# Neighbour slots two at a time: 16-bit words, shift and mask in place of one comparison per slot, and spaced indirect DMAs

## The chip, the core and the metric

The kernel runs on one core of a Trainium2 chip. The metric is the device time of one execution in microseconds (us). Its engines are PE (matmuls), DVE (VectorE), ACT (ScalarE), POOL (GpSimd) and SP (SyncE, which only starts DMAs here).

## The reference

Sixteen graphs of 1024 nodes with 64 channels go through two layers. The first is where the change lies:

```
h = relu(layernorm(x))                           # per node, 64 channels
# drop every skip-th neighbour, and the same edges from the other side
nb   = number of neighbours;  skip = ceil(nb / 2) if nb > 10 else 1
rem  = neighbour and skip > 1 and rank % skip == skip - 1;  rem |= rem.T
nd   = (adjacency with the node itself) and not rem
# per node and channel, over the kept neighbours' h, sorted:
s    = sort(where(nd, h[neighbour], inf));  nv = nd.sum()
agg  = 0.25 * quantile(s, .25) + 0.5 * quantile(s, .5) + 0.25 * quantile(s, .75)   # interpolated
x    = x + mlp(h + agg) * mask                   # 64 -> 128 -> 64
```

The second layer is a layer norm, three graph convolutions `relu(adj @ (x W) + b)` with batch norm, a linear layer over their concatenation, and a residual. A node has some 16 neighbours on average and at most 42 kept ones here; the sort over neighbours is most of the work.

## The kernel before

**Pairs and places.** The graphs are handled in eight pairs, so that 2 x 64 channels fill 128 partitions. `prepare(p)` loads a pair's adjacency, transposes it on PE, drops neighbours, counts each node's kept neighbours (`nv`) and orders the nodes by that count: a node's rank is its *place*. The rows of the adjacency are scattered to DRAM by place (`live_d`, L894, on POOL), read back and transposed (`liveT`). Nodes with like counts then lie next to each other, and ranges of places get a fixed number of neighbour *slots*:

| places | slots | how the neighbours' rows are brought |
|---|---|---|
| block 0: 0 to 200 | 11 | one-hot matmuls |
| block 1: 200 to 392 | 13 | one-hot matmuls |
| block 2: 392 to 640 | 15 | one-hot matmuls |
| NODES: 640 to 768, 768 to 896, 896 to 960 | 17, 19, 21 | indirect DMAs |
| MID: 960 to 1008; tail: 1008 to 1024 | 26; 42 | one-hot matmuls |

**Numbers of neighbours.** At the end of `prepare`, `find_live` multiplies `liveT` with a triangular matrix that has `LIVE` = 128 on its diagonal. In the product `pr` (PSUM, one column a place) a kept neighbour whose rank in its column is k has the value 129 + k, every other node a value under 129. ACT copies the columns of places 0 to 640 (`SPLIT`) as bf16 to `st.r[0]` (L987, once for each of 2 graphs x 8 chunks of 128 nodes and pair: 128 times), and those from 960 on to `st.r[1]` (L1000).

**One-hot gathering.** `gather` takes the slots of a block in groups of as many as fit one PSUM tile (two for blocks 0 and 1, one for block 2). For each slot DVE compares `r` with 129 + slot over all chunks that can hold it:

```
nc.vector.tensor_scalar(                                                    # L1149
    s[:, k, :, us, w0:], r[:, :, us, at + w0 : at + W], float(LIVE + 1 + k0 + k), None, ALU.is_equal
)
```

PE multiplies the features `hp` (h as a sum of three bf16 parts) with that one-hot matrix and adds up over chunks and parts in `pg` (L1180). A place without a neighbour in this slot gets a large number by another product (`none`, L1169 and L1174). ACT copies `pg` to the sorting buffer `g` (L1185). `fewer` (`w0`) leaves out columns in which no node has that slot; where the first product doesn't cover the tile, a product with an identity's zero block clears it (L1159).

**Indirect gathering.** For NODES, lists of row numbers are made (`list_rows`, L711 to L731 on DVE), and `fetch_nodes` issues on POOL one indirect DMA for each slot and half a (L1293; 744 in all, in 20 jobs in the order of `NODE_ORDER`). All jobs but three late ones write into one buffer (tag `gn`), so a job's first DMA waits until the sort of the job before it has read its last. The DMA of the first half (a = 0) also waits for the latest instruction of a sorting network issued so far (`sorted_by`), so that the requests are spread. `list_rows` and all of this precede the sort of the same rows.

**Sorting.** `quantiles` runs a sorting network of DVE minima and maxima (L1087) over `g` and multiplies and adds the quantiles' coefficients (L1099, L1108).

**Order.** `weave(sort, *others)` steps through a sort, and after each part of it issues as many steps of the other generators as are due by the sort's share of work. The number of steps of a gather is what `gather_block` returns. The main loop over p does, in this order: sort block 0 with gathering of block 1 and asking for NODES rows; sort NODES with gathering of block 2; the next fetch, with the sorts of blocks 1 and 2 and gathering of MID and tail; sort NODES; the next fetch, with the sort of MID (`sort_pairs`) and gathering of the next pair's block 0. `prepare(p + 1)` is spread over the first five by `SHARES`. The framework's scheduler then sets each engine's order from this program. After the seventh round, `later` (second layer) is woven with the last pair's sorts: `load` fetches each graph's aggregates back by place with 8 indirect DMAs on POOL (L1486), `first_layer` (L1383) and `next_layer` (L1426 to L1445) follow.

In `load` and in `ask` nothing makes one indirect DMA wait for another, apart from the limited number of semaphores.

Of the kernel before, what the change touches and what calls it, by code (L numbers as in the profile page):

```python
# [13 lines left out]
F8 = mybir.dt.float8e4  # L14
I32 = mybir.dt.int32
U8 = mybir.dt.uint8
U32 = mybir.dt.uint32
AF = mybir.ActivationFunctionType
ALU = mybir.AluOpType
# [388 lines left out]
def graph_layers_kernel(ctx: ExitStack, tc: tile.TileContext, ins, out: bass.AP):  # L408
# [229 lines left out]
    def prepare(p, pools):  # L638


        work, keep, ps = pools
        st = Pair()
        st.p = p
        room = work.tile([P, 4, 2, NT, C], F32, tag="stays", name="room")
        xt, h, sq = room[:, 0], room[:, 1], room[:, 2].rearrange("p x t c -> p (x t) c")
        for x in range(2):
            nc.sync.dma_start(out=xt[:, x], in_=rows_of(x_d[2 * p + x]))
        flat = "p x t c -> p (x t) c"
        layernorm_relu(work, h.rearrange(flat), xt.rearrange(flat), sq, T2)
        for x in range(2):  # L650
            nc.sync.dma_start(out=rows_of(h_d[2 * p + x][:, :]), in_=h[:, x])
            for t in range(4):
                row0 = x * ROWS + 2 + 256 * t
                nc.sync.dma_start(
                    out=rows_d[p][row0 : row0 + 256, :].rearrange("(u j) c -> j u c", j=32),
                    in_=h[32 * t : 32 * t + 32, x],
                )
        yield
        st.g = {}
        st.nvs = keep.tile([P, HELD], BF16, tag="nvs", bufs=2, name="nvs")  # L660
        r0 = keep.tile([P, 2, NT, SPLIT], BF16, tag="r0", name="r0")
        r1 = keep.tile([P, 2, NT, N - REST], BF16, tag="r1", name="r1")
        st.r = (r0, r1)
        rows = {}
        fetch, find_live = [None] * 2, [None] * 2

        def first_rows():
            rows[0] = fetch[0]()

        for x in range(2):  # L670
            fetch[x], find_live[x] = yield from prepare_one(st, x, pools, first_rows if x else None)
        rows[1] = fetch[1]()
        yield
# [12 lines left out]
        nc.vector.tensor_scalar(half, st.nvs, 0.498, MAGIC, ALU.mult, ALU.add)  # L686
        nc.vector.tensor_scalar(half, half, MAGIC, None, ALU.subtract)
        for q, (tau, _) in enumerate(TAUS):
            nc.vector.scalar_tensor_tensor(st.z[:, q, :], st.nvs, -tau, half, ALU.mult, ALU.add)
        yield  # L690

        h = work.tile([P, 2, NT, C], F32, tag="a", bufs=2, name="h_again")
        for x in range(2):
            nc.sync.dma_start(out=h[:, x], in_=rows_of(h_d[2 * p + x][:, :]))
        st.hp = keep.tile([P, 3, 2, NT, C], BF16, tag="hp", name="hp")
        nc.scalar.copy(st.hp[:, 0], h)  # L696
        nc.vector.tensor_tensor(h, h, st.hp[:, 0], ALU.subtract)
        nc.scalar.copy(st.hp[:, 1], h)
        nc.vector.tensor_tensor(st.hp[:, 2], h, st.hp[:, 1], ALU.subtract)
        yield  # L700
        return st
# [62 lines left out]
    def prepare_one(st, x, pools, ahead=None):  # L764
# [156 lines left out]
        def find_live(lp_all, listed):  # L921
# [55 lines left out]
            for u in range(NT):  # L977
                pr = ps.tile([P, N], F32, tag="big", bufs=2, name="pr")
                for a in range(0, SPLIT, HALF):
                    o = slice(a, min(a + HALF, SPLIT))  # L980
                    nc.tensor.matmul(out=pr[:, o], lhsT=upto, rhs=liveT[:, u, o], start=True, stop=(u == 0))
                    if u:
                        nc.tensor.matmul(
                            out=pr[:, o], lhsT=before[:, u : u + 1].to_broadcast([P, P]), rhs=sums[:, o],
                            start=False, stop=True,
                        )
                nc.scalar.copy(st.r[0][:, x, u, :], pr[:, :SPLIT])  # L987
                if u % 2:
                    yield
            def number_rest():  # L990

# [29 lines left out]
    def view(bufs, spec, n1, n2, inner=None):  # L1021

        first, s1, s2 = spec
        buf, base = (bufs[1], first - OTHER) if first >= OTHER else (bufs[0], first)

        def dim(n, s):

            return n, s

        ap = buf[:, base, :]  # L1030
        W = ap.shape[-1]
        t = ap.ap if not callable(ap.ap) else ap.ap()
        part, last = list(t)[0], list(t)[-1]
        dims = [list(part)]
        if n1 > 1:
            dims.append([s1 * W, n1])
        if n2 > 1:
            dims.append([s2 * W, n2])
        if inner is None:
            dims.append(list(last))  # L1040
        else:
            dims += [[s2 * W, n2]] * (n1 == 1 and n2 == 1) + [[inner, W // inner], [1, inner]]
        return bass.AP(tensor=ap.tensor, offset=ap.offset, ap=dims)

    plans = {}
    sorted_by = [None]
# [69 lines left out]
    def per_group(block):  # L1116

        W = block[1] - block[0]
        return max(1, min(HALF // W, 400 // W))

    def gather(st, block, g, pools):


        work, ps, _ = pools
        j0, j1, least, slots = block
        first, end, fewer = NEAR[(BLOCKS + (TAIL,)).index(block)]
        W = j1 - j0
        high = missing_high(slots, least)
        r, at = (st.r[0], j0) if j1 <= SPLIT else (st.r[1], j0 - REST)
        per = per_group(block)  # L1130
        for k0 in range(0, slots, per):
            if k0:
# [85 lines left out]
    def gather_block(st, n, pools, home=None, into=None, first=-0.2, end=0.9):  # L1218


        work, ps, rows = pools
        block = (BLOCKS + (TAIL,))[n]
        j0, j1, _, slots = block
        pool, tag, bufs = home or (rows, f"g{n % 2}", 1)

        def groups():
            if n >= MID:
                z = part_z[n]
                nc.scalar.copy(z[:, :, st.p % z.shape[2], :], st.z[:, :, slice(*held(block))])
            to = into  # L1230
            if to is None:
                to = st.g[n] = pool.tile([P, slots, j1 - j0], F32, tag=tag, bufs=bufs, name="g")
            send(pools, (yield from gather(st, block, to, pools)))
            in_place = n == MID or st.p == NP - 1
            if n >= MID and not in_place:
                nc.scalar.dma_start(out=part_d[n][st.p][:, :, :], in_=to)

        return Steps(groups()), -(-slots // per_group(block)), first, end

    def sort_block(st, n, pools):  # L1240

# [38 lines left out]
    def fetch_nodes(pairs, i, pools, tag):  # L1280
# [7 lines left out]
        def ask():  # L1288
            for k in range(slots):
                for a in range(G):  # L1290
                    st = pairs[a if i == 2 else 0]
                    at = 4 if i == 2 else 2 * a + i
                    asked = nc.gpsimd.indirect_dma_start(  # L1293
                        out=g[:, k, a * C : (a + 1) * C],
                        out_offset=None,
                        in_=rows_d[st.p][:, :],
                        in_offset=bass.IndirectOffsetOnAxis(ap=st.listed[:, at, k : k + 1], axis=0),
                    )
                    if a == 0 and sorted_by[0] is not None:
                        tc.add_manual_dep(  # L1300
                            asked.ins, sorted_by[0].ins.name,
                            mybir.DependencyInfo(mybir.DependencyClass.Sync, mybir.DependencyReason.DATA),
                            reason="rows are asked for one by one",
                        )
                yield

        z = work.tile([P, len(TAUS), G], F32, tag="z_nodes", bufs=2, name="z_nodes")
# [161 lines left out]
    def later(pools, keep, done):  # L1469
# [4 lines left out]
        def load(p):  # L1474
# [5 lines left out]
            for x in range(2):  # L1480
# [2 lines left out]
                nc.sync.dma_start(out=h[:, :, x, :], in_=rows_of(h_d[b][:, :]))  # L1483
                with tc.high_priority():
                    for t in range(NT):
                        nc.gpsimd.indirect_dma_start(  # L1486
                            out=agg[:, t, x, :],
                            out_offset=None,
                            in_=agg_d[b][:, :],
                            in_offset=bass.IndirectOffsetOnAxis(ap=place[:, b, t : t + 1], axis=0),  # L1490
                        )
                nc.sync.dma_start(out=mk[:, :, x], in_=mask_d[b])
            return xt, h, agg, mk

# [329 lines left out]
```

## Time and profile before

| | |
|---|---|
| median of 3 runs | 2872.86 us (2872.21 to 2877.92) |
| profiled execution | 2872.55 us, span 2870.7 us |
| DVE busy | 2347.0 us, 82% of the span |
| PE busy | 2095.5 us, 73% |
| ACT busy | 1584.5 us, 55% |
| POOL busy | 1517.0 us, 53% |
| granted PE clock, mean | 0.88 |

The profile is of one execution. The span runs from its first instruction to its last; the time has some 2 us around it. "Busy" counts an engine's instructions, not its waits. A row of a group reads: line, engine, operation, output <- input with partitions x elements and type, count | busy us, mean ns of one | idle us just before them and what ended that idle time. In the rows of 40 slices each digit is the busy share in tenths of a slice of 71.8 us.

### The profile page before, as it was taken

How to read it: one execution, taken by the hardware profiler on the slowest of the kernel's cores; microseconds unless marked ns; L12 is line 12 of the kernel's file. 1: busy time of each engine (PE TensorE's matmuls, PEld its weight loads, DVE VectorE, ACT ScalarE, POOL GpSimd, SP SyncE). 2: the span in 40 equal slices, each digit the busy share in tenths (PEclk: the TensorE clock that was granted, in tenths of full speed). 3: DMA queues.
4: the chain of work that ended last, by engine and by line, in shares of the span. 5: the costliest groups of instructions: out<-in, count | busy, mean ns of one | idle time of the engine just before them, and what ended most of it. 6: DMA issues, size and time to landing. Idle time of an engine off the chain costs nothing.

```text
span 2870.7 us, 59053 instructions
## 1 busy us (share of the span) xinstructions
PE 2095.5 (73%) x23402; PEld 1450.2 (51%) x23402; DVE 2347.0 (82%) x5475; ACT 1584.5 (55%) x3316; POOL 1517.0 (53%) x1155
## 2 busy tenths in 40 slices
PE   1576986996888688778744985898488396437868
PEld 0344763674565366447522663675366263224545
DVE  3217999999989999999999999999699396637943
ACT  2775776687468568847762687588333133122222
POOL 5115374475838546572834275655855748862220
PEclk9888997998999799889966997999798798768989
DMA  3313222332322242233230322322310341211221
GB/s 98 107 33 103 82 77 58 110 89 65 95 74 73 59 116 86 57 79 99 77 77 12 104 89 74 111 74 64 79 26 14 76 82 52 41 39 45 61 60 46
DMA packets 261055, 205.57 MB, mean 72 GB/s; under 512 B 217121, under 2 KB 217249, under 8 KB 256673
## 3 DMA queue, kind: packets, MB, share of 16 engines
q1 hardware_dynamic: 165120, 131.39, 15.8%
q0 software_dynamic: 39680, 62.23, 9.0%
q10 hardware_dynamic: 55968, 8.09, 1.7%
q8 instruction: 185, 3.03, 0.4%
q14 instruction: 102, 0.83, 0.1%
HBM read 148.82 MB, written 52.75 MB: 70 GB/s over the span
## 4 chain that ended last, share of the span: by engine, by line
DVE 31%; PE 13%; POOL 8%; DMA 8%; ACT 7%; issue 4%; ACTq 0%; POOLq 0%; DVEq 0%; SPq 0%
DVE s L1149 5%; DVE t L1087 4%; POOL g_nodes L1293 4%; PE pg L1441 4%; POOL agg L1486 4%; DVE t_nodes L1087 3%; PE pg L1180 3%; DVE g L1087 2%; DVE g_pairs L1087 2%; DVE t_pairs L1087 2%; DMA a<-in_adj 2%; DVE g_nodes L1087 2%; ACT stays L883 2%; DMA g_nodes<-rows_d,rows_listed 2%; DMA agg<-agg_d,place 2%
## 5 line engine op out<-in xcount | busy, mean ns | idle before, releaser
L1293 POOL DMA_INDIRECT g_nodes<-rows_d,rows_listed x744 | 1123.2, 1510 | 874.4 <-DVE prod L1099 312.5
L1180 PE MATMUL pg<-s,hp 128*64 128x248 bf16 (+6 forms) x12048 | 883.0, 299 | 206.2 <-DVE s L1149 151.1
L1180 PEld LDWEIGHTS <-hp 128*64 128x64 bf16 x12048 | 645.6, 113 | 383.0 <-ACT hp L696 76.4
L1149 DVE TENSOR_SCALAR s<-r 128x3200 bf16<-128x3200 bf16 (+19 forms) x856 | 407.4, 525 | 25.9 <-PE pg L1180 23.7
L1441 PE MATMUL pg<-adjT,xw 128*64 128x512 fp8e4 x2304 | 279.1, 391 | 39.9 <-ACT xw L1430 32.7
L894 POOL DMA_INDIRECT live_d<-edge,place x128 | 189.4, 1480 | 146.9 <-DVE place L886 109.1
L1486 POOL DMA_INDIRECT agg<-agg_d,place x128 | 139.0, 1086 | 190.7 <-DMA agg_d<-agg_nodes 59.1
L1441 PEld LDWEIGHTS <-xw 128*64 128x64 bf16 x2304 | 135.7, 112 | 165.3 <-ACT xw L1430 39.6
L1185 ACT COPY g<-pg 128x248 f32<-128x248 f32 (+3 forms) x238 | 97.0, 408 | 213.1 <-PE pg L1180 212.3
L781 ACT ACTIVATE edge<-a 128x1024 fp8e4<-128x1024 uint32 x128 | 135.5, 1058 | 92.3 <-DMA a<-in_adj 75.5
L788 PE MATMUL ptE<-ident_h,one 128*128 128x128 bf16 x1024 | 84.8, 233 | 114.9 <-DVE one L785 69.2
L1087 DVE TENSOR_TENSOR t<-g 128x800 f32<-128x800 f32 (+9 forms) x184 | 167.5, 923 | 0.8
L1087 DVE TENSOR_TENSOR g<-t 128x992 f32<-128x992 f32 (+7 forms) x176 | 160.2, 931 | 2.0
L864 ACT ACTIVATE edge<-q,bias 128x1024 fp8e4<-128x1024 f32 x128 | 142.2, 1112 | 31.4 <-PE q L859 31.1
L1383 DVE TENSOR_TENSOR agg<-agg,h_late 128x1024 f32<-128x1024 f32 x8 | 9.8, 1229 | 182.2 <-DMA agg<-agg_d,place 182.2
L883 ACT ACTIVATE stays<-keys,minus 128x1024 fp8e4<-128x1024 f32 x128 | 143.1, 1118 | 27.2 <-PE keys L875 26.1
L837 ACT ACTIVATE stays<-cs,back 128x1024 f16<-128x1024 f32 x128 | 137.5, 1113 | 28.3 <-PE cs L833 17.0
L791 ACT ACTIVATE edgeT<-ptE 128x1024 fp8e4<-128x1024 f32 x128 | 131.2, 1028 | 15.5 <-PE ptE L788 14.6
L788 PEld LDWEIGHTS <-one 128*128 128x128 fp8e4 x1024 | 66.0, 104 | 140.2 <-DVE one L785 86.3
L1087 DVE TENSOR_TENSOR t_nodes<-g_nodes 128x256 f32<-128x256 f32 (+6 forms) x192 | 124.2, 658 | 14.4 <-DMA g_nodes<-rows_d,rows_listed 13.8
L929 PE MATMUL pt<-ident_h,lp 128*128 128x128 bf16 x1024 | 88.2, 239 | 58.9 <-ACT liveT L932 30.2
L1445 ACT ACTIVATE xT<-pg,c_L_gnn_b 128x512 f32<-128x512 f32 x48 | 32.9, 686 | 176.6 <-PE pg L1441 176.6
(245 smaller groups left out, 4622.2 us busy)
## 6 DMA issues: line engine op xcount, KB each, us to landing
a<-in_adj SPq DMA_DIRECT2D x128, 512.0 KB
adjT_d<-edgeT SPq DMA_DIRECT2D x16, 1024.0 KB
lp<-live_d POOLq DMA_DIRECT2D x32, 512.0 KB
adjT<-adjT_d SPq DMA_DIRECT2D x16, 1024.0 KB
g_nodes<-rows_d,rows_listed POOLq DMA_INDIRECT x744
room<-in_x SPq DMA_DIRECT2D x16, 256.0 KB
h_d<-room SPq DMA_DIRECT2D x16, 256.0 KB
rows_d<-room SPq DMA_DIRECT2D x64, 64.0 KB
```

The costliest lines, as they stand in the source:

```text
L781: nc.scalar.activation(edge[:, t, :], a[:, :].bitcast(U32), AF.Sign, accum_out=found[:, 0, b, t : t + 1], saturate=False)
L788: nc.tensor.matmul(out=pt[:, u, :], lhsT=one[:, u * P : (u + 1) * P], rhs=ident_h, start=True, stop=True)
L837: nc.scalar.activation(stays[:, t, :], cs, AF.Abs, bias=back[:, t : t + 1], scale=2.0)
L864: nc.scalar.activation(edge[:, t, :], q, AF.Relu, bias=bias(-2.0), accum_out=nv[:, t : t + 1], saturate=False)
L883: nc.scalar.activation(junk, keys, AF.Sign, bias=minus[:, t : t + 1], accum_out=above[:, t : t + 1], saturate=False)
L894: sent = nc.gpsimd.indirect_dma_start(out=live_d[b][:, :], out_offset=bass.IndirectOffsetOnAxis(ap=place[:, b, t : t + 1], axis=0), in_=ed ...
L1087: sorted_by[0] = nc.vector.tensor_tensor(view(bufs, o, n1, n2), view(bufs, a, n1, n2), view(bufs, b, n1, n2), ALU.max if op else ALU.min)
L1149: nc.vector.tensor_scalar(s[:, k, :, us, w0:], r[:, :, us, at + w0 : at + W], float(LIVE + 1 + k0 + k), None, ALU.is_equal)
L1180: summed = nc.tensor.matmul(out=pg[x * C : (x + 1) * C, ks, w0:], lhsT=st.hp[:, part, x, u, :], rhs=s[:, ks, x, u, w0:], start=(whole and ...
L1293: asked = nc.gpsimd.indirect_dma_start(out=g[:, k, a * C : (a + 1) * C], out_offset=None, in_=rows_d[st.p][:, :], in_offset=bass.IndirectO ...
L1441: nc.tensor.matmul(out=pg[cs, :], lhsT=part[:, u, cs], rhs=adjT[x][:, u, sl], start=(u == 0 and k == 0), stop=(u == NT - 1 and k == len(xw ...
L1486: nc.gpsimd.indirect_dma_start(out=agg[:, t, x, :], out_offset=None, in_=agg_d[b][:, :], in_offset=bass.IndirectOffsetOnAxis(ap=place[:, b ...
```

## The change

Four things change.

1. `st.r[0]` holds 16-bit integers. ACT writes `Relu(128 * pr - 256)` to it, rounded to an integer: for a kept neighbour of rank k this is 128 * (127 + k), which is the bit pattern of the bf16 number 2^k. After every second chunk a second ACT instruction reads these words as bf16 and writes them as integers in place: the word is then 1 << k, with 0 or low values for other nodes.
2. Blocks 0 to 2 are gathered by `gather_words`. DVE shifts the words by |k - 3| (right for k over 3, left below) and masks with 0x0808. The low byte is 8 where the rank is k, the high byte where it is k + 8; read as fp8, 8 is 2^-6. One DVE instruction serves slots k and k + 8; slots without a partner keep one instruction each. PE reads every second byte as its moving operand, and ACT's eviction multiplies by 64 (an ACTIVATE with `Copy` and a scale, in place of a COPY). Each block is done in groups of two slots, or one. Full widths are used: `fewer` and the clearing products aren't.
3. In `ask`, the first half's DMA of every odd slot from 3 on waits for the last DMA of the slot before; in `load`, the fifth of eight DMAs waits for the fourth.
4. The step count that `gather_block` gives `weave` becomes slots - 8 + (17 - slots) // 2: 6, 7 and 8 for blocks 0, 1 and 2, where it was 6, 7 and 15.

The tail and MID keep the comparison.

```diff
-        r0 = keep.tile([P, 2, NT, SPLIT], BF16, tag="r0", name="r0")
+        r0 = keep.tile([P, 2, NT, SPLIT], U16, tag="r0", name="r0")
...
-                nc.scalar.copy(st.r[0][:, x, u, :], pr[:, :SPLIT])
+                nc.scalar.activation(
+                    st.r[0][:, x, u, :], pr[:, :SPLIT], AF.Relu, bias=bias(-2.0 * 128.0), scale=128.0
+                )
                 if u % 2:
+                    words = st.r[0][:, x, u - 1 : u + 1, :]
+                    nc.scalar.copy(words, words.bitcast(BF16))
                     yield
...
+    def gather_words(st, block, g, pools):
...
+        groups = [((k,), slice(k, k + 9, 8)) for k in range(slots - 8)]
+        groups += [(tuple(range(k, min(k + 2, 8))), slice(k, min(k + 2, 8))) for k in range(slots - 8, 8, 2)]
+        for at, (shifts, of) in enumerate(groups):
+            if at:
+                yield
+            ks = range(slots)[of]
+            n = len(ks)
...
+            s = work.tile([P, len(shifts), 2, NT, W], U16, tag="s", bufs=2, name="s")
+            for j, k in enumerate(shifts):
+                mine = chunks if len(shifts) == 1 else chunks[j : j + 1]
+                us = slice(min(c.start for c in mine), max(c.stop for c in mine))
+                nc.vector.tensor_scalar(
+                    s[:, j, :, us, :], st.r[0][:, :, us, j0:j1], abs(k - 3), 0x0808,
+                    ALU.logical_shift_right if k > 3 else ALU.logical_shift_left, ALU.bitwise_and,
+                )
+            by_byte = s[:, :, :, :, :].bitcast(F8).rearrange("p j x u (w h) -> p j h x u w", h=2)
+            pg = ps.tile([P, n, W], F32, tag="pg", bufs=3, name="pg")
...
+                those = slice(those[0], those[-1] + 1)
+                for part in range(3):
+                    for x in range(2):
+                        picked = by_byte[:, 0, those, x, u, :] if len(shifts) == 1 else by_byte[:, those, 0, x, u, :]
+                        summed = nc.tensor.matmul(
+                            out=pg[x * C : (x + 1) * C, those, :], lhsT=st.hp[:, part, x, u, :], rhs=picked,
+                            start=(i == 0 and part == 0), stop=(i == len(looks) - 1 and part == 2),
+                        )
+            nc.scalar.activation(g[:, of, :], pg, AF.Copy, scale=64.0)
...
     def gather(st, block, g, pools):
+        if block[1] <= SPLIT:
+            return (yield from gather_words(st, block, g, pools))
...
-        return Steps(groups()), -(-slots // per_group(block)), first, end
+        steps = slots - 8 + (17 - slots) // 2 if j1 <= SPLIT else -(-slots // per_group(block))
+        return Steps(groups()), steps, first, end
...
                     if a == 0 and sorted_by[0] is not None:
-                        tc.add_manual_dep(...)
+                        wait_for(asked, sorted_by[0])
+                    if a == 0 and k % 2 and k > 1:
+                        wait_for(asked, last)
+                    last = asked
...
-                        nc.gpsimd.indirect_dma_start(
+                        asked = nc.gpsimd.indirect_dma_start(
...
+                        if t == 4:
+                            wait_for(asked, last)
+                        last = asked
```

More of the change, by code (lines that the diff above doesn't have):

```diff
@@ L16 @@
 U8 = mybir.dt.uint8
+U16 = mybir.dt.uint16
 U32 = mybir.dt.uint32
@@ L1043, in view, with wait_for @@
         return bass.AP(tensor=ap.tensor, offset=ap.offset, ap=dims)
+    def wait_for(one, other):
+        tc.add_manual_dep(
+            one.ins, other.ins.name,
+            mybir.DependencyInfo(mybir.DependencyClass.Sync, mybir.DependencyReason.DATA),
+            reason="indirect DMAs come with pauses",
+        )
     plans = {}
@@ L1119, in per_group @@
         return max(1, min(HALF // W, 400 // W))
+    def gather_words(st, block, g, pools):
+        work, ps, _ = pools
+        j0, j1, least, slots = block
+        first, end, _ = NEAR[BLOCKS.index(block)]
+        W = j1 - j0
+        high = missing_high(slots, least)
+        groups = [((k,), slice(k, k + 9, 8)) for k in range(slots - 8)]
[5 more added lines that the diff above has]
+            n = len(ks)
+            chunks = [
+                range(
+                    max([c for c in first if k >= first[c]], default=0),
+                    min([c for c in end if k < end[c]], default=NT),
+                )
+                for k in ks
+            ]
+            s = work.tile([P, len(shifts), 2, NT, W], U16, tag="s", bufs=2, name="s")
[5 more added lines that the diff above has]
+                    ALU.logical_shift_right if k > 3 else ALU.logical_shift_left, ALU.bitwise_and,
+                )
+            by_byte = s[:, :, :, :, :].bitcast(F8).rearrange("p j x u (w h) -> p j h x u w", h=2)
+            pg = ps.tile([P, n, W], F32, tag="pg", bufs=3, name="pg")
+            looks = [(u, [i for i in range(n) if u in chunks[i]]) for u in range(NT)]
+            looks = sorted((look for look in looks if look[1]), key=lambda look: -len(look[1]))
+            assert len(looks[0][1]) == n
+            for i, (u, those) in enumerate(looks):
+                if i == 1:
+                    for a, k in enumerate(ks):
+                        if k + 1 not in high:
+                            continue
+                        none = work.tile([P, W], BF16, tag="none", bufs=2, name="none")
+                        nc.scalar.activation(none, st.nvs[:, j0:j1], AF.Relu, bias=bias(k + 0.5), scale=-1.0)
+                        for x in range(2):
+                            half = slice(x * C, (x + 1) * C)
+                            nc.tensor.matmul(
+                                out=pg[half, a], lhsT=ident_big[:, half], rhs=none, start=False, stop=False
+                            )
+                those = slice(those[0], those[-1] + 1)
+                for part in range(3):
+                    for x in range(2):
+                        picked = by_byte[:, 0, those, x, u, :] if len(shifts) == 1 else by_byte[:, those, 0, x, u, :]
+                        summed = nc.tensor.matmul(
+                            out=pg[x * C : (x + 1) * C, those, :], lhsT=st.hp[:, part, x, u, :], rhs=picked,
+                            start=(i == 0 and part == 0), stop=(i == len(looks) - 1 and part == 2),
+                        )
+            nc.scalar.activation(g[:, of, :], pg, AF.Copy, scale=64.0)
+            if 2 * at <= len(groups):
+                halfway = summed
+        st.gathered = summed
+        return halfway
@@ L1128, in gather @@
         high = missing_high(slots, least)
-        r, at = (st.r[0], j0) if j1 <= SPLIT else (st.r[1], j0 - REST)
+        r, at = st.r[1], j0 - REST
         per = per_group(block)
@@ L1299, in ask @@
                     if a == 0 and sorted_by[0] is not None:
[L1300 to L1304, printed above, removed]
+                        wait_for(asked, sorted_by[0])
+                    if a == 0 and k % 2 and k > 1:
+                        wait_for(asked, last)
+                    last = asked
                 yield
```

## The prediction

> **What bounds the kernel now.** I read the busy times and the slices, then the stretch in which the pairs follow each other, then the groups that the change touches, then the waits and the timeline of VectorE and POOL.
>
> ```profile
> PE 2095.5 (73%) x23402; PEld 1450.2 (51%) x23402; DVE 2347.0 (82%) x5475; ACT 1584.5 (55%) x3316; POOL 1517.0 (53%) x1155
> DVE  3217999999989999999999999999699396637943
> POOL 5115374475838546572834275655855748862220
> DVE 31%; PE 13%; POOL 8%; DMA 8%; ACT 7%; issue 4%; ACTq 0%; POOLq 0%; DVEq 0%; SPq 0%
> ```
>
> Each digit is 72 us. VectorE (DVE) shows 9 from the fifth slice to the 28th with one exception, and leads the chain that ended last. The stretch from 500 to 2081 us holds most of the pair loop (columns: length, then busy us of PE, PE's weight loads, DVE, ACT and POOL, granted clock, DMA share, GB/s):
>
> ```profile
> 500.00:2081.00 1581.00, 1213.15 (x14908) 861.61 (x14908) 1503.20 (x3495) 1064.31 (x2246) 911.96 (x597) 0.90 0.30 80
> ```
>
> DVE is busy 1503/1581 = 95%, PE 77%, ACT 67%, POOL 58%. So DVE work that goes away in this stretch shortens it, unless another chain is nearly as long. A steady pair lasts about 250 us (sorting starts of like stages, 240 to 265 apart) with 6 to 18 us of DVE idle in it.
>
> The nearest such chain is POOL's. A fetch of NODES rows fills one buffer; the sort of these rows starts when all have landed; the next fetch starts only when that sort has let the buffer go.
>
> ```profile
> POOL g_nodes L1293 <- DVE prod L1099: 312.5, 9, 48.8
> POOL g_nodes L1293 <- DVE t_nodes L1087: 169.5, 5, 53.8
> DVE t_nodes L1087 <- DMA g_nodes<-rows_d,rows_listed: 13.8, 2, 9.2
> ```
>
> ```profile
> 658.86 1.43 POOL L1293 DMA_INDIRECT g_nodes<-rows_d,rows_listed  x1 [0.30 <-DVE t L1087]
> 662.52 0.41 DVE L1087 TENSOR_TENSOR t_nodes<-g_nodes 128x256 f32<-128x256 f32 x1
> 1039.20 1.20 POOL L1293 DMA_INDIRECT g_nodes<-rows_d,rows_listed  x1 [0.30 <-issue]
> 1049.20 0.42 DVE L1087 TENSOR_TENSOR t_nodes<-g_nodes 128x256 f32<-128x256 f32 x1
> ```
>
> POOL waits 482 us for sorts to end; DVE waits only 13.8 us for rows in the stretch (third line, of 500 to 2081). But the two timeline pairs (last fetch of a job, first sort step on its rows) differ: the first ends at 660.3, rows land about 1.6 us later (median from end to landing over the trace), and the sort starts at 662.5: no room. The second has 8 us of room. Over the 14 jobs of the loop the room is 0, 0, 0, 0.3, 0, 5.3, 6.9, 13.4, 0.1, 13.4, 0, 5.3, 6.8 and 8.4 us. So fetching is a second chain, in half of the jobs as long as DVE's.
>
> **One-hot matrices on DVE (the gain).**
>
> ```profile
> L1149 DVE TENSOR_SCALAR s<-r 128x3968 bf16<-128x3968 bf16 x72 | 86.6, 1203 | 1.5 <-PE pg L1180 1.4
> L1149 DVE TENSOR_SCALAR s<-r 128x3072 bf16<-128x3072 bf16 x80 | 75.3, 959 | 5.2 <-PE pg L1180 5.2
> L1149 DVE TENSOR_SCALAR s<-r 128x3200 bf16<-128x3200 bf16 x64 | 63.0, 987 | 14.2 <-PE pg L1180 12.1 <-ACT r L987 2.1
> L1149 DVE TENSOR_SCALAR s<-r 128x2688 bf16<-128x2688 bf16 x32 | 26.9, 849 | 2.0 <-PE pg L1180 2.0
> ```
>
> With five smaller rows (57.0 us) blocks 0 to 2 have 312 of these, 308.8 us, or 39 and 38.6 us a pair. After the change one instruction serves slots k and k+8: 8 for each block, 24 a pair, on full widths 3200, 3072 and 3968. At the durations above that is 8 x (0.987 + 0.959 + 1.203) = 25.2 us: 13.4 us a pair less. DVE instructions overlap by about 0.08 us at their ends, so 15 fewer of them give back 1.2: 12.2 us a pair, 98 us for eight pairs. One pair's are made ahead of the full stretch; seven lie in it: 85 us.
>
> No uint16 row with shift and mask exists before. From the first two rows, a column costs (1203 - 959)/896 = 0.272 ns, with 122 ns fixed. Best end: the same, 25.2 us. Next: half that rate, 8 x (2.283 + 1.795 + 1.865) = 47.5 us, 8.9 more than before. Worst: a quarter, 92 us. I take the same: source, result and steps have the same widths. The Trainium skill (VectorE: DVE Perf Modes, "What auto-detection actually checks") says the choice looks at widths, steps and memories, not at the operation, but adds that a built-in operation is capped by what the firmware enables. No row shows that for integers, so the half rate stays as a rival.
>
> **ACT.**
>
> ```profile
> L987 ACT CAST r<-pr 128x640 bf16<-128x640 f32 x128 | 87.1, 693 | 28.3 <-PE pr L983 22.2 <-issue 4.4
> L696 ACT CAST hp<-h_again 128x1024 bf16<-128x1024 f32 x8 | 8.3, 1042 | 0.4 <-DMA h_again<-h_d 0.3
> ```
>
> The cast stays one instruction, as ACTIVATE (before, L1445's ACTIVATE of 512 elements from PSUM took 686 ns, L1375's COPY 588): 128 x 0.1 = 13 us. The new conversion to integers has 1280 elements, 64 times; scaling the second row gives 1.25 us: 80 us (bounds: 0.69 us, if the narrower type helps, to 1.9 us). Evictions become fewer by 56 (about -23 us) and the rest ACTIVATE (some 184 x 0.1 = 18 us). Together about 88 us, 11 us a pair: ACT goes from 67% to 72% in the stretch, beside DVE. On the way to the end of prepare, each graph's numbers come about 6 us later; the list work and the pairs' sorts stand in front of their use, and before, DVE waited for `listed` 18.5 us in the whole stretch. If that cover is gone, 12 us a pair. I take 0.
>
> **PE.** Same columns nearly: one-hot columns 3,385,728 before, 3,451,008 after, and 64 identity products fewer.
>
> ```profile
> L1180 PE MATMUL pg<-s,hp 128*64 128x384 bf16 x3408 | 321.2, 334 | 45.2 <-DVE s L1149 21.0 <-ACT coef L1015 20.0 <-ACT o L1214 3.7
> L1441 PE MATMUL pg<-adjT,xw 128*64 128x512 fp8e4 x2304 | 279.1, 391 | 39.9 <-ACT xw L1430 32.7 <-DVE xw L1431 5.0 <-ACT xw L1426 2.0
> ```
>
> The means contain pipeline fill. Start to start in the trace, both types take 0.235 ns a column and 4 ns fixed. 65,280 columns more are +15 us, 2112 matmuls fewer are -9 us: nothing, with PE at 77%. The new operand is bytes of type fp8 at every second byte, which no row shows. Bounds: 0.235 ns a column, or twice that, which would add 800 us to PE and make it the bound. I take the first: the same 16-bit footprint streams at this rate as bf16.
>
> **The pauses on POOL.** As written, odd slots from 3 on wait for the last DMA of the slot before: 156 waits, and 16 in `later`. The Trainium skill (DMA: Bandwidth & Descriptors, "Anatomy of one DMA — SWDGE (gpsimd) path") speaks against this: about 2.0 us fixed for a DMA, mostly its receipt. By that rule 172 x 2.0 = 344 us of POOL standing still, with every later fetch behind it: a slower kernel. In the built program the waits hardly exist. The scheduler puts the second half's DMAs, which have no sort to wait for, between; only 25 such waits are left as instructions, each on the DMA five back, and before, every indirect DMA waited for the one eight back. Four DMAs of 1.2 us plus 0.3 us gaps are 6 us, against 1.6 us to land. So 0 us; upper end 25 x 1.6 = 40 us. POOL's order moves a little (in the late part 28 node DMAs come ahead of the 16 of L1486 instead of 23): 5 x 1.5 = 7 us at most, once or twice; I take 0. DVE's list work (about 14 us a pair) moves from the node stage to the pairs' stage; its sum is unchanged.
>
> **The sum.** POOL's chain limits what of DVE's 85 us arrives. A pair has two fetches. The saving in the window of one is blocks 0 and 1, about 8.9 us of the 12.2, in that of the other block 2, less 1 to 2 us inside the sorting of nodes, 3.5 us. Taking for each job the smaller of saving and room above gives 44 us; 1.4 us inside the node stage of 14 jobs, which shortens both chains, gives 20: 64 us. That is a floor unless POOL stays as slow:
>
> ```profile
> 711.00:745.00 34.00, 22.91 (x246) 15.77 (x248) 34.00 (x105) 11.47 (x28) 32.86 (x4) 0.78 0.19 51
> 2490.00:2523.00 33.00, 2.12 (x19) 0.90 (x15) 0.00 (x0) 0.69 (x1) 24.82 (x27) 0.61 0.15 26
> ```
>
> (Columns as above; all of POOL's work in both is L1293.) With DVE full, 4 fetches took 33 us; with DVE idle, 27 took 25 us. Over the trace a fetch takes 1.57 us with DVE full, 0.95 with it idle. So where DVE would wait for rows, POOL speeds up. I take 67 of the 85 us. The profiled execution took 2872.55 us (span 2870.7), the median of the runs is 2872.86: 2872.6 - 67 = 2806 us.
>
> **The rivals.**
> (1) POOL's chain takes over where there was no room and a moved list or the conversion eats the rest: about 30 us arrive, 2842 us. For it: zero room in seven jobs. Against: POOL's speed when DVE rests. Chance 0.22.
> (2) All of DVE's saving arrives, with that of the first pair: 98 us, 2775 us. For it: DVE waits little for rows. Chance 0.13.
> (3) Slower: shift and mask on 16-bit integers run at half the columns a cycle. Then 7 x 8.9 = 62 us come on top: 2935 us; at a quarter, 7 x 53.6 = 375 us: 3248 us. It decides from 38.6/24 = 1.61 us an instruction. For it: no integer row. Against: widths equal. Chance 0.10.
> (4) The change doesn't do what it says: the pauses are mostly dropped from the program, which my sum has; if they do hold POOL, 40 us of POOL come back and up to 344 by the skill's figure. With the every-second-byte reads on PE, chance 0.09 for slower.
>
> **How the numbers follow.** Likeliest case (2806, own range 2785 to 2825) 0.46; rivals 0.22, 0.13, 0.10, 0.09. A measurement of this kernel tells about 0.2% (5.7 us) from no change. Part of (1) reaches no change: 0.04. Slower: (3), (4) and a bit of (1): 0.20. Faster: 0.76. The range runs from below (2), 2762, to just under no change, 2868, and leaves out the slower cases.
>
> **What would show it.** Right: the uint16 row of width 3968 near 1.2 us; DVE busy near 2347 - 107 = 2240; pair distance near 240; waits of the nodes' sort for rows growing from 13.8 us; POOL's mean of 1510 ns falling; fetches with the same 0.30 us gaps. Wrong: 2.3 us in that row (3); PE rows of 496 columns far above the 384 row's slope; fetches that wait on a DMA for more than 40 us together; DVE waits for `listed` above 60 us.

## The result and the profile after

| | before | changed |
|---|---|---|
| median | 2874.91 us (2872.21 to 2877.92, 4 runs) | 2854.16 us (2849.01 to 2857.68, 4 runs) |
| ratio, 95% interval | 1 | 0.9915 [0.9894, 0.9936] |
| profiled span | 2870.7 us | 2847.2 us |

The change is faster by 21 us, 0.9%, where 67 were forecast. First the profile of the changed kernel: engines' busy time, then the 40 slices of VectorE (DVE).

```profile
PE 2125.1 (75%) x21226; PEld 1371.0 (48%) x21226; DVE 2260.5 (79%) x5356; ACT 1657.1 (58%) x3324; POOL 1361.7 (48%) x1155
DVE  3217999899899989989999999999688486647943
```

Where the old row had a nearly unbroken run of nines, eights are now mixed in. VectorE's busy time fell by 86.5 us (2347.0 to 2260.5), but its idle time in the span grew from 523.7 to 586.7 us, by 63.0. The difference, 23.5 us, is all that the span got shorter. So the question is who makes VectorE wait.

The instruction that was in doubt behaves as the forecast took it (groups by shape on VectorE):

```profile
L1159 DVE TENSOR_SCALAR s<-r 128x3968 uint16<-128x3968 uint16 x64 | 76.6, 1197 | 2.0 <-PE pg L1184 2.0
L1159 DVE TENSOR_SCALAR s<-r 128x3200 uint16<-128x3200 uint16 x64 | 62.3, 993 | 29.0 <-PE pg L1184 28.9
L1159 DVE TENSOR_SCALAR s<-r 128x3072 uint16<-128x3072 uint16 x64 | 60.7, 957 | 24.3 <-PE pg L1184 24.3
```

1197 ns where bf16 with a comparison took 1203. What is new stands at the end of these lines: 55 us of waiting for `pg` on PE (with the tail's and MID's one-hot instructions 69 us), where L1149 had 23.7 in all its shapes. That is 45 of the 63 us. VectorE's largest waits over the span, changed kernel (columns: us in total, times, longest):

```profile
DVE agg L1458 <- DMA agg<-agg_d,place: 175.1, 8, 60.2
DVE s L1159 <- PE pg L1184: 55.2, 28, 6.1
DVE top L712 <- ACT listed L972: 51.1, 11, 21.6
```

The first line belongs to the second layer and was 182.2 us before; the third was 53.1. The wait of the nodes' sort for fetched rows, 13.8 us before, is gone, where the forecast had it grow. POOL's fetch, which the forecast made the limit, isn't one in the pair loop: its mean fell from 1510 to 1320 ns, as forecast, and no sort waits for it.

Now one pair, stage by stage. The first fence is the kernel before, from the end of the second node sort to the first step of block 0's sort of the next pair: the stage in which MID is sorted and block 0 is gathered, then the gap up to block 0's sort. The second is the same of the changed kernel (columns: length, then busy us of PE, weight loads, DVE, ACT and POOL, clock, DMA share, GB/s).

```profile
1202.10:1253.40 51.30, 33.29 (x342) 19.88 (x342) 47.72 (x173) 26.59 (x75) 44.23 (x22) 0.80 0.24 57
1253.40:1256.40 3.00, 2.54 (x63) 1.98 (x59) 3.00 (x9) 0.09 (x1) 2.37 (x3) 1.00 0.34 56
```

```profile
1194.50:1236.60 42.10, 22.04 (x177) 12.55 (x177) 39.51 (x163) 34.59 (x77) 33.21 (x27) 0.62 0.29 62
1236.60:1256.80 20.20, 20.20 (x260) 13.82 (x258) 13.77 (x21) 16.09 (x40) 1.14 (x1) 0.98 0.51 131
```

Before, VectorE was busy 48 of 51 us in the sort of MID, and PE gathered block 0 beneath it; 3 us later block 0's sort began. After, VectorE is through with MID in 42 us, and then 20 us pass in which PE is busy 20.20 of 20.20 and VectorE 13.8. From one block 0's sort to the next VectorE was busy 229.6 us instead of 240.9, but the pair took 246.7 us instead of 248.3 (the forecast: near 240): of 11 us saved, 10 are idle again, 6 of them in this gap.

Two things must be there before PE can gather block 0: the one-hot matrix `s` from VectorE, and `hp`, the split of h with which `prepare` ends. The timelines show which came last. Kernel before:

```profile
1220.49 0.28 DVE L731 TENSOR_TENSOR rows_listed<-top,fill 128x120 int32<-128x120 f32 x1
1220.79 0.99 SPq L694 DMA_DIRECT2D h_again<-h_d  x2
1227.31 0.55 PE L1180 MATMUL pg<-s,hp 128*64 128x400 bf16 x2 [12.76 <-DVE s L1149]
```

Changed kernel, same pair:

```profile
1223.50 0.27 DVE L732 TENSOR_TENSOR rows_listed<-top,fill 128x120 int32<-128x120 f32 x1
1223.80 1.14 SPq L695 DMA_DIRECT2D h_again<-h_d  x2
1228.17 1.05 ACT L697 CAST hp<-h_again 128x1024 bf16<-128x1024 f32 x1 [0.21 <-DMA h_again<-h_d]
1229.27 0.88 PE L1184 MATMUL pg<-s,hp 128*64 128x400 fp8e4 x4 [9.13 <-ACT hp L697]
```

Before, PE stood 12.8 us for VectorE's `s`; now `s` is there first, PE stands 9.1 us for `hp`, and 27 us pass from its first product to block 0's sort. `hp` came no earlier than before (218.1 us after the preceding block-0 sort began, against 216.8), though VectorE had less to do. The lines above it say why: h is reloaded only when VectorE's list work has ended (`rows_listed` is its last instruction). In all eight pairs of both kernels the reload starts 0.03 us after that instruction's end; in the program, it needs a buffer (tag `a`) that the list work holds.

Over the span PE's waits for `hp`, changed kernel:

```profile
PE pg L1184 <- ACT hp L697: 37.0, 4, 9.7
PE pg L1184 <- ACT hp L699: 19.5, 7, 3.8
```

56.5 us, against 26.0 before (17.1 and 8.9); PE's waits for `s` fell from 151.1 to 42.0. The cost to VectorE shows in the stretch from PE's first product with the new `hp` to the first step of block 0's sort. Here are the sums of five such stretches, of all pairs but the first, the last and the one with the tails, in the kernel before and then in the changed one (length, then busy us of PE, weight loads, DVE, ACT and POOL):

```profile
sum 139.00, PE 126.78 PEld 82.97 DVE 136.93 ACT 34.72 POOL 126.20; mean PE 25.36 PEld 16.59 DVE 27.39 ACT 6.94 POOL 25.24
sum 141.90, PE 121.81 PEld 78.35 DVE 105.86 ACT 92.67 POOL 55.65; mean PE 24.36 PEld 15.67 DVE 21.17 ACT 18.53 POOL 11.13
```

The stretches are as long as before, 28 us each, but VectorE stands idle for 36 us in them instead of 2. In the pair with the sort of four tails (1256.8 to 1556.2 us after, 1256.4 to 1575.7 before), where VectorE has 60 us more to sort ahead of block 0, the change did bring 20 us.

### The profile page after: what moved, and what is told of

Same layout as the page of the kernel before. It is cut to its first block, busy times and chain, and to the rows that moved or that the text cites. A ratio compares the mean times of both kernels' runs of the same rounds, so it can differ in the third digit from the quotient of the medians.

```text
span 2847.2 us, 54579 instructions
## 1 busy us (share of the span) xinstructions
PE 2125.1 (75%) x21226; PEld 1371.0 (48%) x21226; DVE 2260.5 (79%) x5356; ACT 1657.1 (58%) x3324; POOL 1361.7 (48%) x1155
## 5 line engine op out<-in xcount | busy, mean ns | idle before, releaser
L1369 POOL DMA_INDIRECT g_nodes<-rows_d,rows_listed x744 | 982.4, 1320 | 951.2 <-DVE prod L1112 282.2
L1184 PE MATMUL pg<-s,hp 128*64 128x496 fp8e4 (+5 forms) x8064 | 745.9, 337 | 131.9 <-DVE s L1159 42.0
L1184 PEld LDWEIGHTS <-hp 128*64 128x64 bf16 x8064 | 449.9, 113 | 373.7 <-ACT hp L697 67.0
L895 POOL DMA_INDIRECT live_d<-edge,place x128 | 182.7, 1427 | 185.6 <-DVE place L887 149.3
L1159 DVE TENSOR_SCALAR s<-r 128x3200 uint16<-128x3200 uint16 (+2 forms) x192 | 199.6, 1049 | 55.3 <-PE pg L1184 55.2
L1561 POOL DMA_INDIRECT agg<-agg_d,place x128 | 129.8, 1014 | 193.6 <-DMA agg_d<-agg_nodes 59.7
L1188 ACT ACTIVATE g<-pg 128x400 f32<-128x400 f32 (+3 forms) x168 | 84.1, 501 | 191.0 <-PE pg L1184 161.1
L930 PE MATMUL pt<-ident_h,lp 128*128 128x128 bf16 x1024 | 107.5, 275 | 60.7 <-ACT liveT L933 34.5
L1255 PE MATMUL pg<-s,hp 128*64 128x384 bf16 (+14 forms) x1872 | 149.4, 302 | 2.7 <-DVE s L1224 2.7
```

The source lines that it names most:

```text
L895: sent = nc.gpsimd.indirect_dma_start(out=live_d[b][:, :], out_offset=bass.IndirectOffsetOnAxis(ap=place[:, b, t : t + 1], axis=0), in_=ed ...
L1159: nc.vector.tensor_scalar(s[:, j, :, us, :], st.r[0][:, :, us, j0:j1], abs(k - 3), 0x0808, ALU.logical_shift_right if k > 3 else ALU.logic ...
L1184: summed = nc.tensor.matmul(out=pg[x * C : (x + 1) * C, those, :], lhsT=st.hp[:, part, x, u, :], rhs=picked, start=(i == 0 and part == 0), ...
L1255: summed = nc.tensor.matmul(out=pg[x * C : (x + 1) * C, ks, w0:], lhsT=st.hp[:, part, x, u, :], rhs=s[:, ks, x, u, w0:], start=(whole and ...
L1369: asked = nc.gpsimd.indirect_dma_start(out=g[:, k, a * C : (a + 1) * C], out_offset=None, in_=rows_d[st.p][:, :], in_offset=bass.IndirectO ...
```

## The experiments

All ratios are to the kernel before on the same chip, run beside it. Where e1 to e11 ran, the kernel before itself took medians of 3118 to 3167 us, with long stops of instruction issue (see e5); where e12 to e18 ran it took 2884 and 2877, as in the first measurement. These groups ran side by side: e1 to e4, e5 to e8, e9 to e11, e12 to e15, e16 to e18.

The expectations name theories. A: the end of `prepare`, with `hp` and the gathering of block 0 on PE, sets a pair's length. B: POOL's fetching does, or still VectorE. C: the pauses hold POOL back. D: the end of `prepare` was the limit before the change already. S: real pauses end the stops. P: real pauses only delay the fetches.

**e14: the changed kernel again.**

> The changed kernel unchanged, as the reference of this call: 1.005 to 1.015 of the kernel before if the stops are there again, 0.99 if they are not.

0.992 [0.9903, 0.9938]: the result holds.

**e5: the same, with the stops.**

> The changed kernel unchanged, so that the three others of this call have it beside them on one chip (the first four runs fell on a chip where the kernel before took 3126 us, against 2873 before, with long stops of instruction issue). All theories: 0.985 to 1.00 of the kernel before.

1.0134 [1.0094, 1.0174]: there the change loses, outside what any theory expected. ACT's largest waits of that kind in this run ("remote": nothing in this core's trace ends the wait; columns: us in total, times, longest):

```profile
ACT g L1188 <- remote: 166.0, 15, 41.3
ACT xT L1520 <- remote: 120.7, 8, 30.3
ACT listed L972 <- remote: 65.4, 4, 23.1
```

In the first profile of the changed kernel ACT has no "remote" wait at all. e1 to e11 are therefore read only against runs of their own group.

**e16: hp earlier, without part 3's waits.** `h_again` is reloaded into a buffer of another tag and split inside `list_rows`, so it stands ahead of the rest of the list work, the second graph's words and the quantiles' terms.

```diff
         for i in range(tiles):
             largest(top[:, i], listed[:, i])
             yield
+        h = work.tile([P, 2, NT, C], F32, tag="byte", bufs=4, name="h_again")
...     # the reload, the two ACT casts and the two DVE differences, moved from the end of prepare
```

> The changed kernel without part 3's waits (0.9885 of the kernel before in e13, 2852 us) and with hp's split ahead of the second graph's words. Theory A (PE's gathering of block 0 waits for hp, 57 us over the run in e13 and e14, and with it the pair): 25 to 55 us less than e13's ratio, 0.970 to 0.980. If prepare's chain is not what sets the pair: 0.986 to 0.991.

0.9767 [0.9746, 0.9787], 2809.5 us: 68 us under the kernel before beside it. The changed kernel without part 3's waits, e13 below, stood at 0.9885 in another group, so the earlier `hp` is worth 34 us. The same stretches of the same pair (sort of MID, then the gap), and the sum of the five stretches from PE's first product to block 0's sort:

```profile
1167.50:1214.20 46.70, 37.40 (x382) 25.86 (x383) 45.01 (x169) 38.65 (x87) 39.30 (x24) 0.83 0.22 52
1214.20:1221.40 7.20, 5.15 (x84) 3.75 (x79) 6.91 (x14) 3.33 (x7) 4.51 (x5) 1.00 0.61 168
sum 133.80, PE 120.97 PEld 92.92 DVE 131.66 ACT 83.48 POOL 96.84; mean PE 24.19 PEld 18.58 DVE 26.33 ACT 16.70 POOL 19.37
```

PE works 37 us beneath the sort of MID instead of 22, and the gap is 7 us instead of 20. In the five stretches VectorE's idle time is 2 us again (35 in e13): about the 34 us that the ratios give. Its waits for fetched rows are 14.6 us, much as the 13.8 before: POOL limits little even here. The profile has VectorE's nines back:

```profile
DVE  3118999899999999999999999999688486657943
```

**e18: the same move in the kernel before.**

> The kernel before with hp's split moved as in e16. Theory A with VectorE as the bound before: 0.995 to 1.00. Rival D (prepare's chain was the bound before the change already): the gain of e16 over e13.

1.005 [1.0032, 1.0067], so no gain, a small loss even. The move that brings the changed kernel 34 us brings the kernel before nothing. In the pair shown above the split now starts at 1196.0 us instead of 1224.9, and PE still waits for VectorE's `s`, as long as without the move:

```profile
1225.05 1.21 PE L1180 MATMUL pg<-s,hp 128*64 128x400 bf16 x6 [12.78 <-DVE s L1149]
```

So `hp` was no limit there, and rival D falls. **e11** was the same with the stops:

> The kernel before with hp's split moved as in e9. Theory A: before the change VectorE is the bound and prepare's chain just fits beside it, so 0.99 to 1.00 of the kernel before, a smaller gain than the same move brings to the changed kernel. Rival D (the chain was already the bound before the change, and VectorE never was): the same gain as in e9, 0.98 or less.

0.9967 [0.9945, 0.999], inside what theory A expected. By itself e11 doesn't exclude D: beside it e9, the changed kernel with the same move, stood at 0.9942, and the changed kernel without the move was not run there.

**e7 and e9: hp earlier with the waits kept, with the stops.**

> The changed kernel with the split of h into hp's three parts moved ahead of the second graph's words (its input is reloaded into another buffer, so it no longer stands behind the list work and the conversions). Theory A: PE waited 9 us for hp in the pair read in the trace, so gathering of block 0 starts up to 9 us earlier in six or seven pairs: 20 to 50 us less than the changed kernel. Theory B: within 6 us of it.

> The changed kernel with hp's split ahead of the second graph's words, once more, for a chip without the long stops of issue that e1 to e8 showed (there the kernel before took 3126 to 3167 us; where it takes 2873 the changed kernel stood at 0.9915 of it). Theory A: 0.975 to 0.985 of the kernel before. Theory B: 0.99 to 0.995.

e7 0.9876 [0.9839, 0.9914], beside 1.0134 for the changed kernel: the direction of e16. e9 0.9942 [0.991, 0.9973] lies where theory B had it, but the chip it met had the stops, and without the changed kernel beside it it settles nothing.

**e17: the words' conversion on VectorE.**

```diff
-                    nc.scalar.copy(words, words.bitcast(BF16))
+                    nc.vector.tensor_copy(words, words.bitcast(BF16))
```

> As e13 with the words' conversion on VectorE: ACT 81 us less, VectorE 29 us more. Theory A: 0.972 to 0.982 of the kernel before. If ACT's conversions lay beside other work, as the forecast had it: 0.989 to 1.00, VectorE being the engine that got more.

0.997 [0.9954, 0.9985], 24 us slower than e13 by the ratios. Theory A named ACT's 81.5 us of conversions as what makes prepare's chain long; that part of it falls. Taking them off ACT didn't shorten PE's wait for `hp` (73.5 us at L697, against 56.7 there in e13): here too the reload of h starts 0.03 us after `rows_listed` in all eight pairs, behind VectorE's list work and not behind ACT. And it put 32.2 us and a wait on VectorE (groups by shape, e17):

```profile
L993 DVE CAST r<-r 128x1280 uint16<-128x1280 bf16 x64 | 32.2, 503 | 14.0 <-ACT r L988 13.1
```

So most of what VectorE gets is still paid (24 of 32 us): it is not off the path, it shares it with the end of `prepare`. With the stops the same edit stood differently:

> The changed kernel with the conversion of the words to integers (64 instructions of 128 x 1280, 81.5 us on ACT) moved from ACT to VectorE. Theory A (the chain of prepare through ACT, then hp, then the gathering of block 0 on PE, is now what sets a pair's length): ACT loses 81 us, VectorE gains some 64 x 0.45 = 29 us, and the time falls by 30 to 50 us below the changed kernel's 2854, to about 2815. Theory B (POOL's fetching of NODES rows is the bound, or VectorE still): no gain, 2854 to 2880, since VectorE only gets more to do.

> As e1, the conversion on VectorE, now beside the changed kernel. Theory A (prepare's chain through ACT sets the pair): 30 to 50 us less than the changed kernel. Theory B (fetching, or VectorE): equal or up to 30 us more.

> The changed kernel with the words' conversion on VectorE, for the same reason. Theory A: 0.975 to 0.985 of the kernel before, as ACT's 81 us leave prepare's chain. Theory B: 0.99 to 1.005.

e1 1.0106 [1.006, 1.0152] and e10 1.0097 [1.0064, 1.013] without the changed kernel beside them, e6 1.0036 [1.0014, 1.0058] beside 1.0134. There, against e5, it gained as theory A expected; the cause of the difference to e17 is open. **e8** had both moves there:

> Both of the last two. Theory A: 50 to 80 us less than the changed kernel, 2775 to 2805 if its 2854 holds: about what the forecast wanted of VectorE's saving. Theory B: equal or up to 30 us more.

0.9943 [0.991, 0.9976]: worse than e7 beside it, so the two don't add up.

**e3: the conversion's cost in the kernel before.** 64 ACT copies of r in place, 128 x 1280.

> The kernel before with 64 extra ACT instructions that copy r in place (128 x 1280, bf16), where the changed kernel converts the words: the suspected cost alone. Theory A: prepare's chain is nearly as long as VectorE's before the change already, so 25 to 45 us more than 2873. Theory B and the forecast's own term: ACT lies beside VectorE's work, within 6 us of 2873.

1.0094 [1.006, 1.0128], 29 us, where ACT's work was to lie beside other work. It ran with the stops and wasn't repeated without; it says that this ACT work isn't free there, no more. It lies in theory A's 25 to 45 us; how it goes with e17, where taking the same work off ACT gained nothing, is open.

**e4: two of hp's three parts.** The second part's products of blocks 0 to 2 are left out.

> The changed kernel with the second of hp's three bf16 parts left out of the products of blocks 0 to 2 (a third of their 8064 matmuls, some 240 us of PE). Theory A: PE is the bound in the gap of some 20 us between the sort of MID and that of block 0, where it gathers block 0; that gap shrinks by some 7 us in seven pairs, to about 2800. Theory B: PE is not on the path, within 10 us of 2854.

0.9794 [0.9741, 0.9847], with the stops and without the changed kernel beside it; e1 and e2, variants of it that ran there, stood at 1.01 and 1.02. So PE is on the path there, in keeping with the gap in which it was busy all of 20.20 us.

**The pauses: none (e13), as built (e14), real (e12).** In e13 the waits are taken out. In e12 an order without a semaphore is kept among the fetches of a job, so that no other DMA is put between and 150 waits are on the DMA directly before:

```diff
+                    if k or a:
+                        tc.add_manual_dep(
+                            asked.ins, last.ins.name,
+                            mybir.DependencyInfo(mybir.DependencyClass.NoSync, mybir.DependencyReason.SCHED_ONLY),
+                            reason="indirect DMAs keep their order",
+                        )
                     if a == 0 and k % 2 and k > 1:
                         wait_for(asked, last)
```

> The changed kernel without part 3's waits, beside the others on one chip. Theory S: the few waits that were left in the changed kernel hardly break POOL's runs, so within 10 us of the changed kernel of this call.

> The changed kernel with an order kept among the fetches of a job, so that the waits of part 3 are on the DMA directly before (150 of them in the program, against 7 in the changed kernel, where most were dropped because a later DMA had been put between). Theory S (the stops of issue on ACT, 20 us and more, come while POOL issues indirect DMAs without a break, and a real pause ends them): ACT's gaps over 5 us fall from some 550-600 us towards the 330 us of the first profile, and the time falls by 100 to 250 us, to 0.93 to 0.98 of the kernel before. Rival P (pauses only delay the fetches): 150 x 1.5 = 225 us more of POOL, of which a third shows, 1.02 to 1.05 of the kernel before.

e13 0.9885 [0.9866, 0.9904], e14 0.992 [0.9903, 0.9938]: as built the pauses cost 8 to 10 us, with intervals that just touch. e12 1.0676 [1.0651, 1.0702], 221 us more than e14, and more than P expected. VectorE's largest waits in e12:

```profile
DVE agg L1464 <- DMA agg<-agg_d,place: 221.7, 8, 90.7
DVE t_nodes L1100 <- DMA g_nodes<-rows_d,rows_listed: 156.5, 18, 22.0
DVE s L1159 <- PE pg L1184: 58.9, 32, 5.8
```

Here is the wait that the forecast expected from POOL's chain: 156.5 us. In the trace of e12 POOL stands 1 to 3 us before 118 of its 744 fetches, 2.2 us in the median; in e14 before 8. So a pause is about as long as the 2.0 us that the Trainium skill (DMA: Bandwidth & Descriptors, "Anatomy of one DMA — SWDGE (gpsimd) path") would charge, and not all of it reaches the time: 221/150 = 1.5 us a pause. The kept order takes part in this number and wasn't measured alone. Theory S, that a real pause ends the stops, couldn't be tried: there were no such stops beside e12. **e2** was e13's kernel on a chip with them:

> The changed kernel without the waits of indirect DMAs for other indirect DMAs (part 3 of the change undone). Theory C (the waits hold POOL back): 20 to 40 us faster than 2854. Theories A and B: within 5 us of 2854, since 25 waits on the DMA five back are all that is left of them in the program.

1.0196 [1.0151, 1.024], without the changed kernel beside it, so it doesn't decide on C. **e15** joined real pauses and the early hp:

> Real pauses and hp's split moved ahead, together. Theory S with theory A: the best of all, 20 to 50 us under e12. Rival P: between e12 and e14.

1.0615 [1.0595, 1.0636]: between e12 and e14, as rival P had it.

## Why the prediction was off

The sign was right and the size was not: -21 us of a forecast -67.

**The step that failed** is "the list work and the pairs' sorts stand in front of their use ... If that cover is gone, 12 us a pair. I take 0", together with "nothing, with PE at 77%". The forecast asked what covers the end of `prepare`, named VectorE's work in that stage, and then removed part of this very work. And it judged PE by its mean over the loop, not in the stage where PE gathers block 0. Before, that gathering waited for VectorE's `s` and ended within VectorE's 51 us; after, VectorE needs 42, `hp` comes no earlier, and PE's 27 us behind it end last. The price of the lost cover stood in the text, up to 12 us a pair, and was set to 0. The runs show 34 us: VectorE's added idle time in five pairs, and what comes back when `hp` is ready earlier (e16), but not in the kernel before (e18). The lateness itself is not what the forecast had in mind, ACT's conversions (e17), but `hp`'s place behind VectorE's own list work. The other 8 to 10 of the 46 us that were missing are the pauses.

The other steps:

- **VectorE's saving** was right in its rows (199.6 us measured for 192 instructions, 201.5 worked out). In busy time it was 86.5 us instead of 98: the durations fell by 111 us in sum, but neighbouring instructions overlap, and with 119 fewer of them 24 us of overlap went too, 0.2 us each and not 0.08. (The forecast's sign "DVE busy near 2347 - 107 = 2240" left even its own 0.08 out; 2260.5 was measured.)
- **ACT's own sums** were right: busy +72.6 us against +88. **PE's rate** for every second byte was right too: 335 ns for the 384-column row, 334 before. PE's busy time rose by 30 us, not 6. The clock granted to it was 0.90 in the forecast's stretch and is 0.88 here (third column from the end, changed kernel, from pair 1's block 0 to pair 7's); whether that is the cause wasn't tried:

```profile
513.60:2063.50 1549.90, 1228.63 (x13238) 801.02 (x13240) 1434.38 (x3400) 1114.27 (x2243) 776.03 (x595) 0.88 0.29 80
```

- **The pauses** were read right from the built program: 8 to 10 us as built, taken as 0 and within the bound of 40 us. From the diff alone they would have been priced at 344 us; made real in e12 they cost 221.
- **"POOL's chain limits what of DVE's 85 us arrives"** was wrong. The room of 0 to 13 us between landing and sort was no limit: fetches got faster when VectorE was less busy, and VectorE's waits for rows went from 13.8 us to none, and to 14.6 in e16. That e16 arrives at 68 us, the forecast's 67, is luck: the forecast took 18 of 85 us off for POOL.
- **Rival (1)** comes nearest, 30 us, and named "a moved list or the conversion" beside POOL. The runs speak for the list, which holds `hp` back, against the conversion's place on ACT (e17), and against POOL. What sets the time of the list itself is open: VectorE waits 51.1 us for `listed` from ACT before it, 53.1 in the kernel before, and the list work wasn't moved by itself. Part 4 of the change and the full widths weren't varied either; e16 has them as they are.

## What to carry to other kernels

When work is taken from the busiest engine, look in each stage for what ran beneath it and ended just in time; its cover goes with the work. Here 86 us were taken from VectorE and 21 arrived, until the split of h was moved ahead (e16, 68 us). And a wait that is written on "the last DMA" costs what the built order leaves of it: 8 to 10 us as scheduled, 221 us once it was real.

## What the runs showed of the hardware

- In eleven runs on three chips (e1 to e11) ACT stood still for 20 us and more at a time with no event in the trace that ends it, and the kernel before took 9 to 10% longer. In e5's three such stops ahead of the copy to `listed` (L972, 20 to 23 us each) VectorE did nothing and PE was busy for 9 to 12% of the time, while POOL, which issued indirect DMAs, was busy for 64 to 75%. The instruction-fetch packets took as long as ever (mean 0.82 us in e5, 0.81 in the first profile of the changed kernel). One of these chips ran e9 to e11 with the stops and e12 to e15 without, so it isn't the chip alone; what makes it happen stays open.
- Shift and mask in one instruction on uint16 run at the rate of a bf16 comparison (1197 and 1203 ns for 3968 columns), and a bf16 to uint16 cast of 1280 columns took 503 ns on VectorE against 1274 on ACT.
